# A 4096-node graph layer whose product A·y is made from seven block products for eight, with the additions on the vector engine and the masks on GpSimd

## The chip, the cores and the metric

The kernel runs on one core of a Trainium2 chip. Such a core has a matrix engine (PE in the profile, with its weight loads as PEld), a vector engine (DVE), a scalar engine (ACT), GpSimd (POOL) and a sync engine (SP), each with its own instruction stream, and 16 DMA engines that serve the queues of SP, ACT and POOL. Engines wait for each other by semaphores; within one engine the instructions run in the order in which they stand. The metric is the device time of one execution in microseconds (us). Time before: 2134.33 us, the median of three runs (2130.61 to 2136.05).

## What is computed

There are N = 4096 nodes with F = 512 features in f32. `adj` is a symmetric pattern with about 0.8% of its entries set and a full diagonal, the values being random and not symmetric.

```
# layer 0
h  = relu(layernorm(x))
d  = rowsum(adj) ** -0.5                      # 0 where the sum is 0
x1 = x + relu((d[:, None] * adj * d[None, :]) @ h @ W0 + b0)
# layer 1
g  = relu(layernorm(x1))
s  = g @ W1 @ a[:F]        t = g @ W1 @ a[F:]
e  = leaky_relu(s[:, None] + t[None, :], 0.2)
P+ = softmax(where(adj > 0, e, -1e12))        P- = -softmax(where(adj > 0, -e, -1e12))
out = x1 + elu(concat([P+ @ g, P- @ g], 1) @ Wtrans)
```

Layer 0 works on `adj` as a dense matrix. Layer 1 uses its pattern: for each block of 64 rows only those columns are gathered that have an entry there.

## The kernel before

**Tiles and groups.** Rows come in 32 tiles of 128. `y0[j] = d_j (h_j W0)` is kept in SBUF for all 32 tiles j. Layer 0 is then `acc_i = sum over j of adj[i, j] y0[j]`, with 128x128 blocks of the transposed `adj` as weights and 512 columns moving. Each f32 matmul is two PE instructions in the profile (two passes), each with its own weight load. The output tiles i are done in eight groups (`GROUPS`, start and count): (26,6), (16,4), (20,4), (0,4), (4,4), (8,4), (12,4), (24,2). I number them 0 to 7. Group 0 runs beside the preparation of `y0` (loading x, layernorm, transposes, the product with W0, the row sums of `adj`) and ends at about 342 us.

**A group (`group`, from line 914).** It goes through jp = 0..15, two tiles j at a time. `load_at` (L780) brings the columns of `adj` on SP's queue, 512 KB at a time: two j for a group of four, four j for the group of two. `multiply` (L790, matmul at L795) issues the products; in the last steps the products are ordered by output tile, so that the accumulators end one after the other. Four PSUM banks hold a group's accumulators, and there are enough banks for two groups.

**Masks (`pack`, L682).** From every `at` tile DVE makes a u8 mask `at > 0` (L692) and the maximum over each 64 columns (`flags`, L696), and POOL's queue writes the mask into tables in DRAM (L708), from which layer 1 gathers. `EARLY` names three groups whose masks are made earlier: in group 2 the tiles of (24,2), in group 3 those of (12,4) and in group 4 those of (8,4) are loaded a first time and masked. So groups 3 and 4 load and mask two tiles each jp, groups 1 and 2 their own (2 also the narrow ones), and 5, 6 and 7 mask nothing.

**Ends of groups (`finish0`, L715).** At jp = 0 of the next group, DVE evicts each accumulator (times d, plus bias), adds x, ACT and DVE make the layernorm `h` (L738 clears its padding on POOL first), two products with the vectors of `a` give s and t (L742), and the row `h` is written into eight tables: one by POOL's queue, seven by ACT's (`put_row`, L420). `h` has two buffers, four for the last but one group, (12,4), whose seven writes per tile are instead kept in `puts` and issued on SP's queue at the end of group 7.

**Lists.** In groups 3 and 5, `make_lists` turns the flags into keys at jp = 2 (`make_keys`), and list rounds on DVE (MAX8 at L375, MATCH_REPLACE at L377) follow, two or three a jp; they give the columns to be gathered. POOL puts the lists together by indirect DMAs (`join`, L390) and deals them out (`deal`).

**Group 7 and the verdict.** Beside the products of (24,2), the first pair of row blocks of layer 1 (pair 16) is begun: `gather0` issues 22 indirect DMAs on POOL (L428) at jp 4, 6 and 10; `weights0` makes the attention weights (scores at L440) and `product0` (L1014) the products. Then `finish0` ends the last two tiles, `judge` (L885) computes a verdict whether the lists hold everything, and a branch on it leads to `sparse_layer1` (L1075). Its PE products are at L1131 and L1154, its gathers again at L428.

**s.** The values of s go to DRAM (`spread_s`, L758) and come back broadcast to all partitions (`load_s`, L768) into eight tiles `s_bc` of 128x512, which stand in SBUF for the whole kernel.

**Order.** The program is written in the order of the work; a scheduler may move instructions of an engine against each other, except those that are held by `keep_in_program_order`. Tiles with several buffers (`bufs`) make a later writer wait for the last reader of the buffer.

Of the kernel before, what the change touches and what calls it, by code (L numbers as in the profile page):

```python
# [27 lines left out]
Y_PARTS = (8, 11, 13)  # L28
EPS = 1e-5
# [228 lines left out]
def gcn_gat_kernel(  # L258
# [21 lines left out]

    nc = tc.nc
# [47 lines left out]
    s_bc = [const.tile([P, 4 * P], F32, name=f"s_bc{k}") for k in range(NJ // 4)]  # L329
# [107 lines left out]
    def scores(r, z, t):  # L437

        n = z.shape[1]
        return nc.vector.tensor_tensor(  # L440
            z,
            t.to_broadcast([P, n, RB]),
            s_bc[r // 8][:, r % 8 * RB : (r % 8 + 1) * RB].unsqueeze(1).to_broadcast([P, n, RB]),
            ALU.add,
        )
# [16 lines left out]
    def tree(pool, r, q, half):  # L462

        t = pool.tile([P, half, 2 * RB], F32, tag="tree", name=f"tree{r}", bufs=1)
# [5 lines left out]
        total = pool.tile([P, 2 * RB], F32, tag="total", name=f"total{r}", bufs=3)  # L470
# [22 lines left out]
    with sbuf(name="y0", bufs=1) as y_pool, sbuf(name="wa", bufs=1) as wa_pool, sbuf(name="bits", bufs=2) as bits_pool, sbuf(name="small0", bufs=4) as small, ExitStack() as lists:  # L493
        list_pool = lists.enter_context(sbuf(name="list", bufs=1))
# [14 lines left out]
        flags = [list_pool.tile([P, EJ * NE, 2 * NH], F32, name=f"flags{g}") for g in range(2)]  # L509
# [7 lines left out]
        xs, hx_t, ars, parts, y0 = {}, {}, {}, {}, {}  # L517
        masks = {}

        def make_keys(g):  # L520
# [3 lines left out]
            kp = []  # L524
            for a in range(2):
                nc.vector.tensor_scalar(bits[:, a], flags[g][:, :, a::2], 0.0, None, ALU.is_gt)
                k2 = ps.tile([P, EN], BF16, tag="ps", name=f"kp{g}_{a}")
                for k in range(EJ):
                    nc.tensor.transpose(
                        k2[:, k * P : (k + 1) * P],  # L530
# [3 lines left out]
                kp.append(k2)  # L534
# [3 lines left out]
            for a in range(2):  # L538
                nc.vector.tensor_tensor(key[:, 2 * a], kp[a], rank, ALU.mult)
            nc.vector.tensor_tensor(key[:, 1], key[:, 0], kp[1], ALU.mult)  # L540
            for a in range(2):
                nc.vector.tensor_tensor(key[:, 2 * a], key[:, 2 * a], key[:, 1], ALU.subtract)
            one = make_pool.tile([P, EN], F32, tag="one", name=f"one{g}")
# [31 lines left out]
        def load_bias():  # L575
            b_row = small.tile([1, F], F32, tag="b_row", name="b_row", bufs=1)
            nc.scalar.dma_start(out=b_row, in_=b0)
            nc.gpsimd.partition_broadcast(b_bc, b_row)
# [13 lines left out]
        def weight_rows(a_sb, w1t):  # L592
# [5 lines left out]
            row = small.tile([2, F], F32, tag="wa_row", name="wa_row", bufs=1)  # L598
# [17 lines left out]
        def load_x(ln_pool, queue, j):  # L616
# [627 lines left out]
```

## Time and profile before

| | us |
|---|---|
| median of three runs | 2134.33 (2130.61 to 2136.05) |
| the profiled execution | 2154.16 |
| its span, first to last instruction | 2152.4 |
| PE busy in the span | 2071.5 |
| DVE, ACT, POOL busy | 1040.5, 409.4, 945.2 |
| products of layer 0 (L795), busy | 891.8 |
| products of layer 1 (L1131 and L1154), busy | 767.2 and 225.1 |
| last product of group 7 ends | 1057.7 |
| verdict | 1071.96 |
| first product of layer 1 | 1126.33 |

A row of the profile names the line, the engine, the operation, output and inputs, shape and type, the number of instructions, the busy time and the mean of one in ns, and then the idle time of that engine just before them with what ended it. Times of matmuls overlap, since they are pipelined, so PE's rate is read from the distance between starts rather than from the duration of one. In windows, each engine's busy time in a stretch stands with its number of instructions, then the granted PE clock as a share, the share of the DMA engines' time and GB/s. A wait is given as engine, output and line, what released it, total us, how often, and the longest. In a timeline, the start, the duration, and in brackets the idle time before with its releaser.

### The profile page before, as it was taken

What the parts mean: (1) busy time and instruction counts of PE and PEld (TensorE: products, weight loads), DVE (VectorE), ACT (ScalarE), POOL (GpSimd) and SP (SyncE); (2) the same over time, 40 slices, a digit from 0 to 9 for tenths busy, and PEclk for the clock granted to TensorE, in tenths of its full rate; (3) what the DMA queues carried; (4) which work ended last, traced back from release to release, by engine and by line L of the source; (5) the groups of instructions that cost most, each with busy time, mean ns of one, the idle gap of its engine ahead of it and who ended that gap; (6) DMA issues with size and microseconds to landing.
All of it is one profiled execution on the core that took longest, in us unless ns stands there. A gap on an engine that the chain in (4) does not pass through costs nothing.

```text
span 2152.4 us, 17006 instructions
## 1 busy us (share of the span) xinstructions
PE 2071.5 (96%) x5208; PEld 938.0 (44%) x5208; DVE 1040.5 (48%) x2429; ACT 409.4 (19%) x764; POOL 945.2 (44%) x1017
## 2 busy tenths in 40 slices
PE   7999999999999999999849999999999999999998
PEld 3443444444444444444324444444444444444443
DVE  5444524243498638912414635455444454454441
ACT  5545610000000000000112222112212212112111
POOL 2010002121213230232376677777777777777740
PEclk9999999999999999999979999999999999999999
DMA  9988928887865966283888878887878887888850
GB/s 367 372 303 327 359 91 302 260 289 227 303 223 198 309 207 222 83 268 126 296 260 261 255 231 250 245 241 240 246 239 241 249 240 236 244 246 241 244 172 21
DMA packets 186427, 523.86 MB, mean 243 GB/s; under 512 B 25683, under 2 KB 34995, under 8 KB 186326
## 3 DMA queue, kind: packets, MB, share of 16 engines
q0 software_dynamic: 73856, 283.61, 43.5%
q1 hardware_dynamic: 81728, 183.20, 24.7%
q10 hardware_dynamic: 30742, 55.88, 7.4%
q8 instruction: 42, 0.69, 0.1%
q14 instruction: 59, 0.48, 0.1%
HBM read 419.67 MB, written 102.92 MB: 243 GB/s over the span
## 4 chain that ended last, share of the span: by engine, by line
PE 85%; DMA 5%; issue 4%; DVE 2%; ACT 1%; POOL 1%; another core or an unknown queue 1%; DVEq 0%; POOLq 0%; ACTq 0%
PE u L1131 35%; PE acc L795 35%; PE o L1154 10%; DMA xt<-in_x 4%; PE yp L657 2%; PE tp L486 1%; PE u L1014 1%; DVE sta L410 0%; ACT ar L647 0%; DMA ar<-in_adj 0%; PE cs L476 0%; POOL g L428 0%; DMA ld<-dummy 0%; DMA g<-table,idx 0%
## 5 line engine op out<-in xcount | busy, mean ns | idle before, releaser
L795 PE MATMUL acc<-y,at 128*128 128x512 f32 x2048 | 891.8, 593 | 2.4 <-ACT y L680 2.4
L428 POOL DMA_INDIRECT g<-table,idx x704 | 751.6, 1068 | 281.6 <-issue 198.0
L1131 PE MATMUL u<-g,p 128*128 128x512 f32 x1736 | 767.2, 599 | 16.8 <-DVE p L460 12.1
L795 PEld LDWEIGHTS acc<-y,at 128*128 128x128 f32 x2048 | 385.8, 190 | 474.8 <-issue 469.3
L1131 PEld LDWEIGHTS u<-g,p 128*128 128x128 f32 x1736 | 327.2, 191 | 407.6 <-issue 393.2
L440 DVE TENSOR_TENSOR z<-g,s_bc 128x512 f32<-128x512 f32 (+1 forms) x128 | 79.6, 623 | 392.4 <-DMA g<-table,idx 357.3
L1154 PE MATMUL o<-wt_sb,ut 128*128 128x512 f32 x512 | 225.1, 592 | 0.5 <-ACT ut L490 0.5
L460 DVE SCALAR_TENSOR_TENSOR p<-g,p 128x384 f32<-128x384 uint8 (+1 forms) x256 | 143.4, 620 | 76.4 <-issue 40.6
L692 DVE TENSOR_SCALAR m<-at 128x1024 uint8<-128x1024 f32 (+2 forms) x142 | 88.5, 632 | 159.7 <-DMA at<-in_adj_t 154.2
L453 ACT ACTIVATE p<-z 128x896 f32<-128x896 f32 (+2 forms) x136 | 116.0, 903 | 203.2 <-issue 114.6
L708 POOL DMA_DIRECT2D table<-m x71 | 54.9, 774 | 226.2 <-DVE m L692 188.0
L657 PE MATMUL yp<-w_sb,hx_t 128*128 128x512 f32 x256 | 123.4, 628 | 19.9 <-ACT y L680 17.9
L1154 PEld LDWEIGHTS o<-wt_sb,ut 128*128 128x128 f32 x512 | 94.8, 190 | 107.8 <-issue 106.9
L1140 ACT ACTIVATE us<-u,rl 128x512 f32<-128x512 f32 x62 | 42.6, 687 | 447.6 <-issue 277.9
L390 POOL DMA_INDIRECT ld<-li,off x48 | 45.2, 942 | 160.0 <-DMA ld<-li,off 104.0
L647 ACT ACTIVATE ar<-ar 128x1024 f32<-128x1024 f32 x96 | 100.1, 1043 | 17.9 <-DMA ar<-in_adj 17.9
L657 PEld LDWEIGHTS yp<-w_sb,hx_t 128*128 128x128 f32 x256 | 50.7, 201 | 88.6 <-issue 60.5
L610 ACT ACTIVATE rrb<-rrb 128x1 f32<-128x1 f32 x32 | 5.9, 199 | 417.3 <-DVE rrb L609 352.8
L618 POOL DMA_DIRECT2D xt<-in_x x28 | 15.8, 565 | 153.9 <-ACT hx L614 129.2
L375 DVE MAX8 lst<-keys 128x8 f32<-128x512 f32 x120 | 79.4, 682 | 0.9
L377 DVE MATCH_REPLACE8 keys<-lst,keys 128x512 f32<-128x512 f32 x114 | 76.4, 673 | 0.0
L449 DVE SCALAR_TENSOR_TENSOR z<-z 128x896 f32<-128x896 f32 (+2 forms) x68 | 70.8, 1041 | 2.2
(149 smaller groups left out, 1058.0 us busy)
## 6 DMA issues: line engine op xcount, KB each, us to landing
at<-in_adj_t SPq DMA_DIRECT2D x136, 512.0 KB
ar<-in_adj SPq DMA_DIRECT2D x128, 512.0 KB
table<-h ACTq DMA_DIRECT2D x182, 258.0 KB
table<-m POOLq DMA_DIRECT2D x55, 256.0 KB
at<-in_adj_t SPq DMA_DIRECT2D x32, 384.0 KB
g<-table,idx POOLq DMA_INDIRECT x704
xr<-in_x POOLq DMA_DIRECT2D x32, 256.0 KB
x1d<-y POOLq DMA_DIRECT2D x32, 256.0 KB
```

Source lines behind the costliest of these rows:

```text
L375: nc.vector.max(top, keys[:, c, :])
L377: nc.vector.match_replace(keys[:, c, :], top, keys[:, c, :], 0.0)
L428: nc.gpsimd.indirect_dma_start(out=gt[:, k, :], out_offset=None, in_=table[2 * n // RPT], in_offset=bass.IndirectOffsetOnAxis(ap=idx[n // ...
L440: return nc.vector.tensor_tensor(z, t.to_broadcast([P, n, RB]), s_bc[r // 8][:, r % 8 * RB : (r % 8 + 1) * RB].unsqueeze(1).to_broadcast([ ...
L453: nc.scalar.activation(p[:, :, g, :], z, AF.Exp, scale=(1.0, -1.0)[g])
L460: nc.vector.scalar_tensor_tensor(e, m, 0.0, e, ALU.is_gt, ALU.mult)
L647: i = nc.scalar.activation(ar, ar, AF.Identity, accum_out=part[:, c : c + 1])
L657: nc.tensor.matmul(yp, hx_t[j][:, c * P : (c + 1) * P], w0_sb[:, c, :], start=c == 0, stop=c == FC - 1,)
L692: i = nc.vector.tensor_scalar(m, at, 0.0, None, ALU.is_gt)
L795: nc.tensor.matmul(a, at[:, c, it * P : (it + 1) * P], y0[j0 + c], start=j0 + c == 0, stop=j0 + c == NJ - 1,)
L1131: nc.tensor.matmul(u, p[:, k0 + k].rearrange("p g c -> p (g c)"), gt[:, k, :F].bitcast(F32), start=k0 + k == 0, stop=k0 + k == nk - 1,)
L1154: nc.tensor.matmul(po, ut[:, g, c, :], wt_sb[:, g * FC + c, :], start=g == 0 and c == 0, stop=g == 1 and c == FC - 1,)
```

## The change

**Products.** For groups 1 to 7, two tiles j and two tiles i make a 2x2 block problem: the blocks of `adj` are 128x128, and each `y0` tile is cut into two halves of 256 columns. `multiply_blocks` makes seven products of 256 columns in place of eight. Their operands are the blocks themselves and sums of them: `sum_at` makes four sums on DVE for each `at` tile, and `sum_y` makes four per jp once, in group 1 (it also alters the y0 tiles in place and fills `t` tiles). The results stand in 3.5 banks per column pair, seven banks for a group of four; `join_blocks` makes the output tiles from them at the group's end: one ACT copy and five DVE additions per pair, then the affine step in the old eviction's place. Group 0 keeps the plain products.

**Masks.** In groups 1 to 6 `pack` makes the mask by POOL's `tensor_scalar`; the maximum stays on DVE and is issued one step later. The flags are bf16.

**Buffers and order.** The `at` buffers are six in all in place of nine and two; in group 7 four in place of five. The `h` of (12,4) has three buffers in place of four. One tile is finished per jp (order 0, 2, 1, 3), and x for it is loaded beforehand. List rounds are two a jp (three in group 6), joins one a jp. In group 7 the gathers' parts 1, 2 and 0 come at jp 4, 7 and 10, in place of 2, 1 and 0 at jp 4, 6 and 10.

**s.** The `s_bc` tiles are gone. `s_pair` (for pair 16) is loaded on ACT's queue at jp 0 of group 7; in layer 1 `load_s` brings 256 KB for four pairs at a time on SP, two of them ahead of `wt_sb`.

```diff
-    s_bc = [const.tile([P, 4 * P], F32, name=f"s_bc{k}") for k in range(NJ // 4)]
...
-        def pack(i0, j0, at, pin=False):
+        def pack(pool, engine, i0, j0, at, pin=False):
...
-            i = nc.vector.tensor_scalar(m, at, 0.0, None, ALU.is_gt)
+            i = engine.tensor_scalar(m, at, 0.0, None, ALU.is_gt)
...
-            nc.vector.tensor_reduce(
+            return partial(
+                nc.vector.tensor_reduce,
...
+        def join_blocks(i0, n, acc, work):
+            ys = {}
+            for x in range(n // 2):
+                p16, p23, p45, p7 = acc[x]
+                j0, j1 = i0 + x, i0 + n // 2 + x
+                ys[j0], ys[j1] = y, v = [new_y(work, j, -1) for j in (j0, j1)]
+                w = work.tile([P, H], F32, tag="w", name=f"w{j0}", bufs=1)
+                nc.scalar.copy(y[:, :H], p16[:, :H])
+                nc.vector.tensor_tensor(w, p16[:, H:], y[:, :H], ALU.add)
+                nc.vector.tensor_tensor(y[:, H:], p45[:, H:], w, ALU.add)
+                def first(p23=p23, y=y):
+                    nc.vector.tensor_tensor(y, p23, y, ALU.add)
+                def second(p7=p7, w=w, p45=p45, v=v):
+                    two = "p (a f) -> p a f"
+                    nc.vector.tensor_tensor(w, p7, w, ALU.add)
+                    nc.vector.tensor_tensor(
+                        v.rearrange(two, a=2), p45.rearrange(two, a=2),
+                        w.unsqueeze(1).to_broadcast([P, 2, H]), ALU.add)
...
+        def sum_y(jp):
+            k = 0 if jp < T_PARTS[0] else 1
+            t = ty[jp] = t_tiles[k][:, jp - k * T_PARTS[0]]
+            ya, yb = y0[2 * jp], y0[2 * jp + 1]
+            sub = partial(nc.vector.tensor_tensor, op=ALU.subtract)
+            sub(t[:, 1], yb[:, H:], ya[:, H:])
+            sub(ya[:, H:], ya[:, H:], ya[:, :H])
+            sub(t[:, 0], yb[:, H:], ya[:, H:])
+            sub(t[:, 2], yb[:, :H], t[:, 0])
+        def sum_at(pool, at, n, name):
+            a = blocks_of(at, n)
+            q, w = a.shape[1], a.shape[4]
+            t = pool.tile([P, 4, q, w], F32, tag="sums", name=name)
+            op = nc.vector.tensor_tensor
+            op(t[:, 0], a[:, :, 0, 1], a[:, :, 1, 1], ALU.add)
+            op(t[:, 1], t[:, 0], a[:, :, 0, 0], ALU.subtract)
+            op(t[:, 2], a[:, :, 0, 0], a[:, :, 0, 1], ALU.subtract)
+            op(t[:, 3], a[:, :, 1, 0], t[:, 1], ALU.subtract)
+            return t
+        def multiply_blocks(acc, n, jp, at, t):
...
+            for x in range(n // 2):
+                p16, p23, p45, _ = acc[x]
+                product(x, p16[:, :H], a[:, q, 0, 0], ya[:, :H], True)
+                product(x, p16[:, H:], t[:, 1, q], s[:, 0], False)
+                product(x, p45[:, :H], a[:, q, 1, 1], s[:, 2], True)
+                product(x, p45[:, H:], t[:, 0, q], ya[:, H:], False)
+                product(x, p23[:, :H], a[:, q, 1, 0], yb[:, :H], True)
+                product(x, p23[:, H:], t[:, 3, q], yb[:, H:], False)
+                if not last:
+                    seventh(x)
...
-        def group(b, work, at_pool, early, step):
+        def group(b, work, at_pool, sum_pool, step, prod, n_h=2):
...
-            for jp in range(NJ // 2):
+            prepare(0)
+            for jp in range(NP):
+                if jp + 1 < NP:
+                    prepare(jp + 1)
                 if jp == 0:
-                    finish0(work, *pending)
-                    acc = [bank(f"acc{i0 + k}") for k in range(n)]
...
+                    ys = take(work)
+                    p7 = bank(f"p7_{i0}")
+                    acc = [
+                        [*(bank(f"p{k}_{i0 + x}") for k in (16, 23, 45)), p7[:, x * H : (x + 1) * H]]
+                        for x in range(n // 2)
+                    ]
+                multiply_blocks(acc, n, jp, ats[jp], sums[jp])
+                while marking:
+                    marking.pop(0)()
...
+                        marking.append(pack(bits_pool, nc.gpsimd, e0, 2 * jp, at))
+                if jp < pn:
+                    j = order[jp]
+                    h = work.tile([P, ROW_W], F32, tag="h", name=f"h{j}", bufs=n_h)
+                    finish0(work, j, ys.pop(j), h, prod)
...
-        with sbuf(name="work0", bufs=2) as work, sbuf(name="at", bufs=9) as at_pool, sbuf(name="early", bufs=2) as early:
+        with sbuf(name="work0", bufs=2) as work, sbuf(name="sums", bufs=3) as sum_pool, sbuf(name="at", bufs=6) as at_pool:
...
-                    for _ in range((2, 3)[b % 2 == 0] if jp > 2 else 0):
+                    for _ in range((2, 3)[b == 6] if jp != 2 else 0):
                         if listing:
                             listing.pop(0)()
+                    if joining:
+                        joining.pop(0)()
...
-        with sbuf(name="work2", bufs=2) as work, sbuf(name="at2", bufs=5) as at_pool, ...
+        with sbuf(name="work2", bufs=2) as work, sbuf(name="sums2", bufs=2) as sum_pool, sbuf(name="at2", bufs=4) as at_pool, ...
...
                 if jp == 4:
+                    gather0(1)
+                if jp == 7:
                     gather0(2)
-                if jp == 6:
-                    gather0(1)
...
-            group(len(GROUPS) - 1, work, at_pool, None, step)
+            group(len(GROUPS) - 1, work, at_pool, sum_pool, step, row_tile, 3)
...
+            wanted = list(dict.fromkeys(r // 8 for r in order))
+            for _ in range(2):
+                tc.keep_in_program_order(load_s(wanted.pop(0)))
             for a in range(3):
                 gather1(pairs[0], a)
...
                     weights(order[k + 2])
+                    if wanted and order[k + 2] % 8 == 7:
+                        load_s(wanted.pop(0))
```

## The prediction

> **What bounds the kernel now.** I read the busy shares first, then the chain that ended last, the windows by group, and the rows and waits at the places that the change touches. The shares and the chain's sum by engine:
>
> ```profile
> PE 2071.5 (96%) x5208; PEld 938.0 (44%) x5208; DVE 1040.5 (48%) x2429; ACT 409.4 (19%) x764; POOL 945.2 (44%) x1017
> PE 85%; DMA 5%; issue 4%; DVE 2%; ACT 1%; POOL 1%; another core or an unknown queue 1%; DVEq 0%; POOLq 0%; ACTq 0%
> ```
>
> PE is the bound. The changed stretch, groups 1 to 7 of layer 0, runs from about 341.7 us (end of group 0) to 1057.7 us. The chain there, and windows of groups 3 and 6 (PE, PEld, DVE, ACT, POOL busy, clock, DMA share, GB/s):
>
> ```profile
> 399.78 110.06 PE acc L795 x256
> 954.13 80.90 PE acc L795 x188
> ...
> 547.00:659.00 112.00, 112.00 (x286) 49.67 (x285) 88.20 (x221) 4.22 (x9) 20.78 (x33) 1.00 0.76 256
> 881.00:992.00 111.00, 111.00 (x261) 48.91 (x260) 37.66 (x95) 4.18 (x9) 29.13 (x42) 1.00 0.53 169
> ```
>
> 256 passes (each f32 matmul is two) take 110.06 us: 0.43 us each, no gap, at full clock. Seen from here, time falls one for one with PE's work until another engine is late. DVE has 24 us to spare in the fullest group, 73 in the emptiest. The rows I price with:
>
> ```profile
> L795 PE MATMUL acc<-y,at 128*128 128x512 f32 x2048 | 891.8, 593 | 2.4 <-ACT y L680 2.4
> L486 PE MATMUL tp<-ident,us 128*128 128x128 f32 x256 | 39.5, 278 | 18.1 <-issue 18.1
> L468 DVE TENSOR_TENSOR tree<-tree 128x256 f32<-128x256 f32 x64 | 26.7, 417 | 1.2
> L692 DVE TENSOR_SCALAR m<-at 128x1024 uint8<-128x1024 f32 x94 | 64.9, 697 | 140.9 <-DMA at<-in_adj_t 135.5 <-DMA table<-m 5.3
> L325 POOL CAST ident<-ident 128x128 bf16<-128x128 f32 x1 | 0.3, 280 | 0.0
> L496 POOL IOTA rank<- 128x512 f32 x1 | 0.6, 556 | 10.2 <-issue 10.2
> L708 POOL DMA_DIRECT2D table<-m x71 | 54.9, 774 | 226.2 <-DVE m L692 188.0 <-DVE mva L414 14.8 <-DVE rs L670 6.9
> ```
>
> **Step 1: PE's products.** Each pair of row tiles has 13 column pairs over the groups, 16 steps jp. Before: 13x16x8 = 1664 passes of 512 columns; the starts lie 0.4289 us apart, 713.7 us in all. After: 13x16x7x2 = 2912 passes of 256. No row has that width. The durations of 512 and 128 columns give a slope of (593-278)/384 = 0.82 ns a column; half of 0.4289 is 0.2145. I take 0.2155. The weight loads could forbid it: they take 190 ns each, but
>
> ```profile
> 1305.70 0.30 PEld L476 LDWEIGHTS cs<-ones,total 128*128 128x128 f32 x2
> ```
>
> shows two inside 0.30 us, so a new one may start after 0.11 us. Bounds: 0.2145 below, 0.297 (half of the whole duration) above; the period of 512 is the nearest row, so I stay low. 2912x0.2155 = 627.5 us: 86.2 saved, 79.5 in the six groups of four (109.8 to 96.5 us each, 6.03 a jp) and 6.6 in the last group. At the upper bound the products would take 865 us.
>
> **Step 2: DVE's adds.** A group of four gets 16 times four 256-column adds (start to start about 0.335 us): 1.4 us of each 6.03, 23 a group. sum_y adds the same once, all in group 1. The join adds per column pair one ACT copy and five DVE adds (three at 417, two 512 wide at 685 ns) in place of nothing; the affine takes the old eviction's place: +5 us a group. The masks leave DVE: 96 of 1024 (0.6 start to start) and 16 of 512, 32 of the large in each of groups 3 and 4, 16 in 1 and 2. Demand per group against 96.5 us of PE, in group 3: sums 23, join and affine 8, finish 4x3.3 = 13, 32 flags at 0.32 = 10, keys 8, 26 list rounds at 1.27 (a MAX8 of 682 ns, a load, a replace of 673) = 33: 95. The like gives about 80 in group 1 (six tiles, sum_y), 58 in 2, 92, 90 and 87 in groups 4 to 6 (up to 30 rounds, no masks in the last two). On average it fits. But DVE works in order: make_keys with the first rounds is a block of about 10 us at jp 2, and the last finish's dot waits for table writes (14 to 15 us from one put to the next that may follow, h having two buffers):
>
> ```profile
> DVE prod L742 <- DMA table<-h: 22.0, 3, 11.2
> POOL h L738 <- DMA table<-h: 77.5, 15, 8.3
> ```
>
> Before, nothing that PE needed stood behind these on DVE except evictions; now sum_at of the next pair does, and three buffers of sums (12 us) are its slack. Following program order, group 3's sums for jp 5 come about 5 us late, and in groups 4 to 6 the fourth tile's dot ahead of the sums for jp 5 or 7 costs 2 to 5 us each. I take 18 us for groups 1 to 6. Bounds: 0 to 3 if the writes land sooner, 60 if groups 3 to 6 run at DVE's rate with these waits uncovered (10 to 15 each).
>
> **Step 3: masks on POOL.** The trace has none. The nearest rows: CAST 128 columns in 280 ns, IOTA 512 in 556: 0.72 ns a column above the start, so 1024 take 0.9 us; 8x280 = 2.24 is the other end. I take 1.2. POOL in group 4 then has 32x1.2 + 16 mask writes x0.77 + about 20 us of rows and joins = 71 of 96.5: covered. The cover ends at 2.0 us a mask there and 2.3 in group 3. At 2.24 group 4 runs 8 us long; the flags reduce on DVE, which waits for the mask, then stalls the sums behind it. Below nothing: no gain beyond DVE's 64 us, counted already.
>
> One rule speaks against this step. DVE's 417 ns add was measured with no GpSimd arithmetic beside it. The Trainium skill, page "SBUF — State Buffer", section "SBUF: two separate sides", says that a DVE instruction with two SBUF inputs and a GpSimd instruction that reads SBUF exclude each other for the whole instruction. No row of this trace shows such a pair. By it 32 masks would hold the adds up by an estimated 0.4 us each, 13 us in each of groups 3 and 4, and the sum below would end some 20 us later.
>
> **Step 4: groups' ends, buffers, transfers.** The acc banks had been double; now seven of eight are one group's. The first column pair's join (2.6 us) lies beside the second pair's products of the last step only if DVE is on time; 0 to 1 us per boundary, in step 2's 18. The at buffers fall from 9+2 to 6, one load per jp (two in groups 3 and 4, three in flight ahead). The same bytes in 12% less time lift the DMA share from 0.76-0.86 to 0.87-0.98 (group 0 held 0.99), so loads need not be late; if in group 1 they are, 0 to 5 us. xr is loaded earlier on POOL: no wait. Joins, one a jp, only spread POOL's issues.
>
> **Step 5: the last group and the verdict.** Here I expect a loss. Three lines of before:
>
> ```profile
> 1009.51 0.54 POOL L420 DMA_DIRECT2D table<-h  x1 [2.67 <-issue]
> 1015.15 1.02 POOL L428 DMA_INDIRECT g<-table,idx  x1 [5.10 <-DMA table<-h]
> 1045.06 21.89 SPq L420 DMA_DIRECT2D table<-h  x28
> 1071.96 0.15 DVE L911 CAST verdict<-ok_ps 1x1 int32<-1x1 f32 x1 [0.28 <-PE ok_ps L908]
> ```
>
> The group starts at 1002.3; gathers of pair 16 start 12.9 us in, and the verdict falls 69.7 in. With h's buffers cut from four to three, h of tile 15 on POOL must wait for the seven table writes of the first tile (12). Those are on SP behind the load of the last at tiles, whose buffer is free when PE ends jp 7, about 24 us in. Seven writes of 0.78 us: issued and written at about 33. Then POOL makes h15, its put and (5.1 us later, as before) the first gather: 41 us in instead of 12.9. Queued behind h15 on POOL are all 22 gathers: 22x1.25 = 27.5, landing 6 to 7 later, at about 75; the weights from them stand on DVE ahead of the last verdict steps: verdict about 80 us in. So the 6.6 us of this group go, and 10.5 are added after them. Bounds: -6.6 if the writes land with the 24 and the gathers' chain is slack, +15.
>
> **Step 6: s in layer 1.** The 32 broadcasts that stood on ACT and SP in layer 0 go; a 256 KB load per four pairs comes on SP. The first two stand ahead of wt_sb (landed 1123 before, needed later) and weights(34) waits for one. Gathers take the time from verdict to 1126.33 anyway, so I take +2, bounds 0 to 8.
>
> **Sum.** -79.5 + 18 + 10.5 + 2 = -49 us. The profiled execution took 2154.16 us (span 2152.4), 20 above the median of 2134.33: the sum makes 2105 of it, and 2085 of the median.
>
> **Rivals.** (A) PE's stream is everything: DVE slack and the gathers' cover hold. -86 +0 to 6 gives 2048 to 2054. For it: averages of every engine fit. Against: in-order waits above. (B) DVE becomes the bound in groups 3 to 6 (95, 92, 90, 87 of 96.5 are a hair from it): step 2 at 40 to 60, and step 5's loss: 2105 to 2130. (C) Slower, by GpSimd: masks of 3 us and over make POOL the bound, since groups 3 and 4 hold 32 each: 64m+22+33 against 193 us, an excess of 54 us at m = 3.0, where the gain is gone, 86 at 3.5: about 2170. Against: no elementwise row of POOL is near 3 ns a column. (D) The change does not do what it says: a 256-column pass costs no half of a 512. At 0.245 us 2912 of them take 713.7 again; then step 5's and 6's loss makes it 2140 to 2147, and 0.26 some 2185. For it: PE spends 44% of its time in weight loads, and their number grows by 1.75. Against: the 0.30 row.
>
> **How the numbers follow.** Less than 0.3% (6.4 us) can't be told from no change here. Forecast, 2060 to 2105: 0.45. A: 0.14. B: 0.15. Between B and no change, 2128 to 2141: 0.05. C: 0.12, D: 0.09. Faster 0.74, same 0.05, slower 0.21. The range 2050 to 2150 reaches from A through B and the bottom of D; outside it lie the most of C, half of D and a little of A: under 0.2. The likeliest alone: 2060 to 2105.
>
> **What the profile after would show.** Step 1: one PE row of 256-column products, x2912 where none is missing, starts 0.215 apart, groups of 96 to 100 us. Step 2: PE's idle on DVE sums in groups 3 to 6, a few us each; DVE busy above 85 of 97 there. Step 3: POOL masks of 1.0 to 1.5 us, with flags waiting little; adds at 417 ns, longer if the rule holds. Step 5: the first gather of pair 16 about 40 us into the last group, after a POOL wait for table writes; the verdict 10 us later against its start. Step 6: layer 1's first weights waiting for s or not. The forecast is wrong if masks exceed 2 us, if a pass exceeds 0.23, or if PE's idle time in groups 3 to 6 is under 2 us in all.

## Result

The changed kernel takes 2301.77 us, the median of four runs (2292.57 to 2303.65), against 2132.47 us of the kernel before on the same chip: a ratio of 1.0785, 95% interval 1.0750 to 1.0821. It is 169 us slower where 49 us less were forecast. The profiled execution has a span of 2301.7 us; that of the kernel before, 2152.4 us, was taken from an execution some 20 us above its median, so the two spans lie 149 us apart and not 169.

The page's busy times and the chain by engine, of the changed kernel:

```profile
PE 2062.9 (90%) x6456; PEld 1212.3 (53%) x6456; DVE 1186.8 (52%) x2862; ACT 414.7 (18%) x779; POOL 1234.2 (54%) x1129
PE 41%; POOL 5%; DMA 4%; issue 2%; DVE 2%; ACTq 0%; ACT 0%; SPq 0%; DVEq 0%; POOLq 0%
```

PE was 96% busy and 85% of the chain; it is now 90% and 41% (the shares add up to little over half of the span, since the chain can be followed back only to 1049.6 us). Windows by group, for groups 1, 2, 4, 5 and 6 (columns as before: PE, PEld, DVE, ACT, POOL busy, clock, DMA share, GB/s); the boundaries are the ACT copies of the last join of each group, and group 3, from 593.4 to 753.1, is left out:

```profile
341.00:455.00 114.00, 101.63 (x444) 86.24 (x443) 67.87 (x189) 6.33 (x15) 69.26 (x56) 0.96 0.70 237
455.00:593.40 138.40, 112.89 (x451) 93.13 (x450) 54.63 (x151) 5.00 (x11) 83.54 (x61) 0.89 0.58 184
...
753.10:931.30 178.20, 122.18 (x452) 99.31 (x452) 98.28 (x253) 5.09 (x12) 115.88 (x77) 0.80 0.55 182
931.30:1032.50 101.20, 100.12 (x477) 85.33 (x476) 89.92 (x246) 4.83 (x11) 14.87 (x24) 1.00 0.59 191
1032.50:1141.30 108.80, 100.88 (x452) 86.46 (x451) 71.03 (x199) 4.96 (x11) 31.99 (x43) 0.95 0.49 159
```

The groups that make masks (1 to 4) take 114, 138, 160 and 178 us against 110 before; 5 and 6, which make none, take 101 and 109. No engine fills the slow groups: in group 4, the slowest, DVE is busy for 98 of 178 us, POOL for 116, and the DMA engines' share is 0.55. So the groups are held up by waits that follow each other in a ring. The groups of instructions that carry it, shapes kept apart:

```profile
L690 POOL TENSOR_SCALAR m<-at 128x1024 uint8<-128x1024 f32 x94 | 262.0, 2792 | 146.4 <-DMA at<-in_adj_t 135.5 <-DVE sums L854 5.8 <-DVE lst L376 3.9
L1037 DVE TENSOR_REDUCE flags<-m 128x16 bf16<-128x256 int32 x88 | 36.2, 412 | 183.2 <-POOL m L690 163.9 <-POOL h L779 19.4
L864 PE MATMUL p<-t,sums 128*128 128x256 f32 x832 | 267.1, 406 | 90.4 <-DVE sums L852 81.8 <-DVE sums L853 8.5
```

A mask on GpSimd takes 2.79 us. GpSimd waits 136 us for at tiles, DVE 164 us for masks, PE 90 us for sums: each for the one before. One turn of the ring in group 4, from the timelines of SP, POOL, DVE and PE:

```profile
842.68 0.88 SPq L811 DMA_DIRECT2D at<-in_adj_t  x2
848.30 0.87 POOL L391 DMA_INDIRECT ld<-li,off  x1 [4.49 <-DMA ld<-li,off]
849.24 2.80 POOL L690 TENSOR_SCALAR m<-at 128x1024 uint8<-128x1024 f32 x1
852.07 0.42 DVE L1037 TENSOR_REDUCE flags<-m 128x16 bf16<-128x256 int32 x1 [4.98 <-POOL m L690]
853.13 2.80 POOL L690 TENSOR_SCALAR m<-at 128x1024 uint8<-128x1024 f32 x1
855.97 0.42 DVE L1037 TENSOR_REDUCE flags<-m 128x16 bf16<-128x256 int32 x1 [1.35 <-POOL m L690]
857.69 0.41 DVE L851 TENSOR_TENSOR sums<-at 128x256 f32<-128x256 f32 x1
858.83 1.22 PE L864 MATMUL p<-t,sums 128*128 128x256 f32 x2 [4.04 <-DVE sums L852]
855.96 0.88 SPq L811 DMA_DIRECT2D at<-in_adj_t  x2
```

The last line is the next turn's pair of loads. SP issues two loads at 842.68. GpSimd is kept by a join that waits 4.49 us for the one before it, makes two masks, DVE takes flags from each as it comes, and only then stands the next step's sums; PE gets them at 858.83. The second mask, ended at 855.93, frees an at buffer, and SP issues the next two loads at 855.96. The turn is 13.3 us for a step that PE does in 6.03. In group 4 SP waited 80.1 us, 14 times, for masks before it issued loads.

What links the ring is the order of DVE's queue. The program names the flags of a step behind the sums of two steps later. As built they stand ahead of older sums. In group 2, the flags of step 2 (by the loads that the mask and the sums read) stand ahead of the last of the four sums of step 0:

```profile
448.70 0.42 DVE L1037 TENSOR_REDUCE flags<-m 128x16 bf16<-128x256 int32 x1 [3.00 <-POOL m L690]
449.04 0.48 DVE L854 TENSOR_TENSOR sums<-at,sums 128x256 f32<-128x256 f32 x1
```

In the turn of group 4 above, the two flags stand ahead of all four sums of the step that PE needs next, and the first of them belongs to the step after it (the second is of a tile that is marked only). The tile that the first marks sits in one of six buffers, whose last holder must be done first, so PE waits for a load, two masks and the flags for tiles that it needs only later or not at all. Whether more `at` buffers would have hidden the mask's price was not tried.

Each wait costs more than its length. PE's windows behind such a wait, in group 4 (the first pair of passes after a wait of 7.42 us starts at 822.27):

```profile
822.30:826.50 4.20, 4.20 (x10) 3.40 (x11) 2.43 (x6) 0.00 (x0) 1.25 (x1) 0.50 0.79 258
827.50:830.50 3.00, 3.00 (x15) 2.47 (x13) 2.45 (x7) 0.00 (x0) 3.00 (x2) 1.00 0.01 3
```

The granted clock is 0.50 for some 4 us after an idle time of 7.42 us, ten passes in 4.2 us, and 1.00 after that. Over all runs with block products, 94 of the 105 waits of 3.1 us or more in the products are followed by a first pair of 1.1 us or more (1.22 us is half clock), and 9 of the 55 waits of 1.5 to 3.1 us; 40 of these 55 by one of 0.70. The Trainium skill has this, page "TensorE: Matmul & The Clock Gate", section "Part 1: The HAM clock gate (the "warmup" mystery)": an idle window of about 3.4 us halves the clock until PE has been busy for about as long. The runs agree with it in the main.

The sum of the stretch of groups 1 to 7: 859.0 us = 627.5 (2912 passes at 0.2155) + 150.0 of idle time before products + 81.5 of rest. By the clock records of the trace PE was busy for 115 us of this stretch at a granted clock below full, which makes some 57 us of the rest; 66 small products make some 4, and the other 20 are not assigned. Of the idle time, 107.5 us are waits for sums and 35.8 for the first add of a join (`w`, four waits, the longest 16.4 us). Before it was 716. After its end the verdict comes 31.0 us later (14.3 before), and from the verdict to the end it is 1070.8 us (1080.4 before). So 143 of the 149 us between the two spans lie in the stretch.

### The profile page after: what moved, and what is told of

Same layout as the page of the kernel before. It is cut to its first block, busy times and chain, and to the rows that moved or that the text cites. A ratio compares the mean times of both kernels' runs of the same rounds, so it can differ in the third digit from the quotient of the medians.

```text
span 2301.7 us, 20151 instructions
## 1 busy us (share of the span) xinstructions
PE 2062.9 (90%) x6456; PEld 1212.3 (53%) x6456; DVE 1186.8 (52%) x2862; ACT 414.7 (18%) x779; POOL 1234.2 (54%) x1129
## 4 chain that ended last, share of the span: by engine, by line
PE 41%; POOL 5%; DMA 4%; issue 2%; DVE 2%; ACTq 0%; ACT 0%; SPq 0%; DVEq 0%; POOLq 0%
PE u L1279 27%; PE o L1302 8%; POOL g L429 5%; PE p L864 3%; DMA g<-table,idx 2%; PE tp L484 1%; DMA table<-h 1%; PE u L1149 1%; ACTq L421 0%; DMA xr<-in_x 0%; PE cs L474 0%; DMA ld<-li,off 0%; DVE z L441 0%; DVE prod L783 0%; PE u L1161 0%
## 5 line engine op out<-in xcount | busy, mean ns | idle before, releaser
L690 POOL TENSOR_SCALAR m<-at 128x1024 uint8<-128x1024 f32 (+1 forms) x110 | 286.1, 2607 | 153.3 <-DMA at<-in_adj_t 142.2
L864 PE MATMUL p<-t,sums 128*128 128x256 f32 x832 | 267.1, 406 | 90.4 <-DVE sums L852 81.8
L864 PE MATMUL p<-y,sums 128*128 128x256 f32 x832 | 267.4, 405 | 17.2 <-DVE sums L854 17.2
L864 PE MATMUL p<-y,at 128*128 128x256 f32 x832 | 263.3, 400 | 6.4 <-DVE y L749 5.0
L864 PEld LDWEIGHTS p<-t,sums 128*128 128x128 f32 x832 | 166.4, 204 | 127.2 <-DVE sums L852 93.2
L864 PEld LDWEIGHTS p<-y,sums 128*128 128x128 f32 x832 | 169.2, 204 | 46.5 <-DVE sums L854 20.1
L864 PEld LDWEIGHTS p<-y,at 128*128 128x128 f32 x832 | 167.4, 203 | 36.3 <-DVE y L749 7.1
L823 PE MATMUL acc<-y,at 128*128 128x512 f32 x384 | 176.5, 598 | 2.4 <-ACT y L678 2.4
L864 PE MATMUL p<-t,at 128*128 128x256 f32 x416 | 134.2, 406 | 36.0 <-DVE w L745 35.8
L823 PEld LDWEIGHTS acc<-y,at 128*128 128x128 f32 x384 | 71.0, 191 | 81.2 <-issue 78.0
```

The costliest lines, as they stand in the source:

```text
L690: i = engine.tensor_scalar(m, at, 0.0, None, ALU.is_gt)
L823: nc.tensor.matmul(a, at[:, 0, it * P : (it + 1) * P], y0[j], start=j == 0, stop=j == NJ - 1)
L864: i = nc.tensor.matmul(out, left[:, x * P : (x + 1) * P], right, start=jp == 0 and first, stop=jp == NP - 1 and (final or not first),)
```

## Experiments

The medians of the kernel before lay at 2132, 2151, 2151, 2151 and 2131 us in the sets of runs below, which were made on several chips; so each is compared by its ratio to the kernel before on the same chip.

### Masks back on DVE

```diff
-                    marking.append(pack(bits_pool, nc.gpsimd, i0, 2 * jp, ats[jp]))
+                    marking.append(pack(bits_pool, nc.vector, i0, 2 * jp, ats[jp]))
-                        marking.append(pack(bits_pool, nc.gpsimd, e0, 2 * jp, at))
+                        marking.append(pack(bits_pool, nc.vector, e0, 2 * jp, at))
```

> The changed kernel with the masks of groups 1 to 4 back on DVE, all else kept. Theory (the mask on GpSimd, 2.79 us each, with DVE's flags waiting for it in order, is what costs): DVE gets 19 us of masks back in groups 3 and 4 and 10 in groups 1 and 2, which makes it the bound at 112 to 115 us in 3 and 4; the groups take about 102, 100, 115 and 112 us in place of 114, 138, 160 and 178, so some 160 us go: about 2140 us. Rival (the sums' place in DVE's order and the six at buffers cost the time, whoever makes the masks): groups 3 and 4 stay at 140 us or more: 2200 or more.

Measured: 2168.94 us, ratio 1.0076 (1.0043 to 1.0108); groups 1 to 4 at 103, 113, 116 and 117 us. The theory's size was nearly met (it named 2140 on the first chip, a ratio of 1.003): nine tenths of the loss hangs on who makes the masks. But the kernel isn't faster than before. Group 2 has little work on DVE and still takes 113 us. Timeline of DVE in it:

```profile
513.75 0.69 DVE L690 TENSOR_SCALAR m<-at 128x1024 uint8<-128x1024 f32 x1 [4.01 <-DMA at<-in_adj_t]
514.82 0.41 DVE L851 TENSOR_TENSOR sums<-at 128x256 f32<-128x256 f32 x1
521.02 0.69 DVE L690 TENSOR_SCALAR m<-at 128x1024 uint8<-128x1024 f32 x1 [4.00 <-DMA at<-in_adj_t]
522.08 0.42 DVE L851 TENSOR_TENSOR sums<-at 128x256 f32<-128x256 f32 x1
```

Each step, DVE waits 4 us for the load of a tile that it needs now for its mask only, with this step's sums behind it (the tile's own sums come two steps later, by the order of the loads): the same ring with a shorter link, 7.3 us a step instead of 6.03.

### Masks on ACT

```diff
-            i = engine.tensor_scalar(m, at, 0.0, None, ALU.is_gt)
+            if engine is nc.scalar:
+                i = nc.scalar.activation(m, at, AF.Relu, scale=100.0)
+            else:
+                i = engine.tensor_scalar(m, at, 0.0, None, ALU.is_gt)
```

and `nc.scalar` in the two calls of `pack`.

> The changed kernel with the masks of groups 1 to 4 made by ACT (relu of 100 times the entry into u8, which is above 0 just where the entry is, entries lying in 0.05 to 1). Theory: ACT is busy 4 to 7 us a group; 32 masks at about 1.05 us (its 1024-column row) make 34: groups 1 to 4 at about 100 us each, so 190 us go: about 2110 us. Rival (ACT's queue is late, since its layernorm steps wait up to 20 us for table writes and the masks stand behind them, so flags and at buffers are late): groups 3 and 4 at 125 or more, 2150 to 2200 us.

Measured: 2167.89 us, ratio 1.0060 (1.0024 to 1.0095); groups 1 to 4 at 101, 110, 122 and 109. Neither expectation was quite met: it lies between them. A mask on ACT takes 1.05 us, ACT is busy for 24 to 38 us of these groups, and DVE has none of the masks' work left; yet the stretch takes 714.5 us against 716.7 with the masks on DVE. So the masks' work on DVE is not what bounds it.

### The kernel before, with its masks on GpSimd

```diff
-            i = nc.vector.tensor_scalar(m, at, 0.0, None, ALU.is_gt)
+            i = (engine or nc.vector).tensor_scalar(m, at, 0.0, None, ALU.is_gt)
```

with `engine=nc.gpsimd` in groups 1 to 4, and the flags one step later.

> The kernel before with only the masks of groups 1 to 4 moved to GpSimd, the flags on DVE issued one step later as in the change. Theory: 32 masks of 2.79 us and 22 to 33 us of other POOL work make 111 and 122 us in groups 3 and 4 against 110 of PE, but nothing that PE needs waits for POOL except through at buffers and evictions: 2135 to 2155 us. Rival (GpSimd masks cost as much by themselves as in the changed kernel, through at buffers that come free late): above 2200 us. Second rival (they hurt only beside the sums): 2133 us.

Measured: 2273.85 us, ratio 1.0549 (1.0506 to 1.0591). The theory fell, and so did the second rival; the first rival's size was met (by the ratio the time is 2250 us on the first chip, where it named more than 2200). The masks on GpSimd cost some 118 us, by the ratio, without any block product or sum. The flags were not held here, so how much of this is the price and how much the order is not separated. In the waits, and in PE's timeline:

```profile
DVE flags L935 <- POOL m L692: 286.2, 85, 27.7
```

```profile
674.17 0.62 PE L553 MATMUL o_ps<-count,before 128*16 128x3 f32 x18 [24.19 <-DVE count L546]
```

Here no sums stand behind DVE's waits, but the list work does, and PE has small products for the lists in its own queue among the large ones: 24 us in that one line. The `at` buffers come free late too, as the first rival has it: SP waited 344 us for masks between 335 and 1180 us, though PE only 18 us for `at` tiles. The links through which a late mask reaches PE are others, the late mask is the same.

### Flags one step later in the program

```diff
-                while marking:
-                    marking.pop(0)()
+                late_marks, marking = marking, []
+                while waiting:
+                    waiting.pop(0)()
+                waiting.extend(late_marks)
...
```

with one mask buffer more for it, two of the lists' tiles sharing theirs.

> The changed kernel, masks on GpSimd, but the flags of a step are issued one step later still (one mask buffer more for it, two of the lists' tiles sharing theirs). If the link from GpSimd to PE is DVE's in-order wait for the mask ahead of the sums, that wait has a step (6 us) more of slack and most of the stall in groups 1 and 2 and a third or more in 3 and 4 goes: 2210 to 2250 us. If POOL's own rate or the release of at buffers by the masks is the link, nothing changes: 2290 to 2305 us.

Measured: 2320.09 us, ratio 1.0775 (1.0744 to 1.0806). No change, and no test either: in group 2 the scheduler put the flags at the same places in DVE's queue, ahead of the last sum of two steps before, and in groups 3 and 4 ahead of the sums as well. It led to the next edit, which holds the order.

### The order held, with the masks on GpSimd, DVE and ACT

```diff
                 while marking:
-                    marking.pop(0)()
+                    tc.keep_in_program_order(marking.pop(0)())
```

(for DVE the masks too).

> The changed kernel, masks on GpSimd, but every flags instruction held on DVE in the order of the program, so behind the sums of the step after next instead of ahead of the sums two steps older (the scheduler had moved it there, and the run with later flags had left that order as it was). Theory (the loop buffer free, load, mask on GpSimd, flags, sums, products is what stretches a step): groups 1 to 4 fall from about 114, 138, 160, 178 us to 101, 103, 113, 124, the last two by GpSimd's own rate: some 150 us less than the changed kernel's ratio of 1.0785 to before, so a ratio near 1.01. Rival (GpSimd's rate and its late release of at buffers alone): ratio 1.055 or more.

> Masks on DVE as in the earlier run with them there, masks and flags held in the order of the program, behind the sums of the next step. If the order was what was left, group 2 falls from 113 to 98 and groups 3 and 4 to DVE's demand of 111 to 114 from 116 and 117: 20 to 25 us less, ratio 0.997. If DVE is simply full: no change, ratio 1.007.

> Masks on ACT as in the earlier run with them there, flags held in the order of the program. Theory (order): groups 1 to 4 from 101, 110, 122, 109 to 98, 98, 104, 102: about 40 us less, ratio 0.988. Rival (something else than the flags' place keeps the sums late, ACT's masks behind its waits for table writes or the lists): ratio 1.00 to 1.006.

Measured, with the two unheld runs for comparison (groups and stretch in us, of the profiled executions; PE's idle time before products, and the rest beyond it and 627.5 us of passes):

| masks on | order | ratio to before | groups 1 to 4 | stretch | PE idle | rest |
|---|---|---|---|---|---|---|
| GpSimd (the change) | scheduler's | 1.0785 (1.0750 to 1.0821) | 114, 138, 160, 178 | 859 | 150 | 82 |
| GpSimd | held | 1.0328 (1.0278 to 1.0379) | 112, 97, 132, 164 | 775 | 94 | 53 |
| DVE | scheduler's | 1.0076 (1.0043 to 1.0108) | 103, 113, 116, 117 | 717 | 52 | 38 |
| DVE | held | 1.0053 (1.0027 to 1.0079) | 105, 97, 113, 124 | 707 | 39 | 40 |
| ACT | scheduler's | 1.0060 (1.0024 to 1.0095) | 101, 110, 122, 109 | 715 | 51 | 36 |
| ACT | held | 0.9905 (0.9873 to 0.9938) | 101, 98, 116, 112 | 695 | 35 | 33 |

With the masks on GpSimd, the order alone is worth 4.6%, about 98 us, less than the 150 expected and more than the rival allows, since groups 3 and 4 stay at 132 and 164. There the rival's link shows: in group 4 SP waits 110 us, 16 times, for masks before it issues loads, and PE 11.9 us for `at` tiles themselves. Group 2 becomes nearly free of PE's waits for sums and takes 97 to 98 us in all three, 96.5 of them its passes. With the order held and the masks on ACT the kernel is faster than before: 2135.53 us against 2150.79, the best of all, though by under 1%. That is the forecast's sign, at less than half its size (20 us of 49, by the ratio). With the masks on DVE no gain is shown, as the two intervals overlap: group 2 falls to 97 us, but groups 3 and 4 take 113 and 124, of which DVE is busy for 97 and 105.

### Four buffers of h in the last group

On top of the masks on ACT with the order held:

```diff
-            group(len(GROUPS) - 1, work, at_pool, sum_pool, step, row_tile, 3)
+            group(len(GROUPS) - 1, work, at_pool, sum_pool, step, row_tile, 4)
```

> As the run before it, and four buffers of h in the last group instead of three. If the wait of the fourth tile's h for the first one's seven table writes is what moves the gathers of pair 16 and the verdict, the first gather starts some 15 us into the last group instead of 50, the verdict falls 70 to 75 us in instead of 90, and the time falls by 12 to 18 us more: ratio 0.981. If the gathers were covered anyway: no change against the run before it.

Measured: 2135.68 us, ratio 0.9923 (0.9898 to 0.9948): no change. The mechanism that the prediction named is there. In the changed kernel POOL's timeline has

```profile
1183.17 0.10 POOL L779 MEMSET h<- 128x3 f32 x1 [20.80 <-DMA table<-h]
1185.22 0.54 POOL L421 DMA_DIRECT2D table<-h  x1 [1.94 <-DVE prod L783]
1191.68 1.02 POOL L429 DMA_INDIRECT g<-table,idx  x1 [5.92 <-DMA table<-h]
```

50 us into the group that starts at 1141.3; with four buffers it is

```profile
997.34 1.22 POOL L429 DMA_INDIRECT g<-table,idx  x1 [2.55 <-PE p L867]
```

26 us in (start at 971.0). But the verdict falls only from 89.9 to 85.3 us after the group's start, PE's last group is 70 us instead of 61, and from the verdict to the end it takes 1076.7 us instead of 1074.0; of the earlier gathers nothing is left in the medians. The longer group holds four waits of PE, 9.3 us in all, before which the profile shows nothing that released it, and the other run's group has none of them; what made them is not shown.

### GpSimd's prices

Beside group 6 of the kernel with the masks on ACT and the order held, six instructions on 512 columns, four times each:

```diff
...
+                        if kind < 3:
+                            nc.gpsimd.tensor_scalar((u8, f32, bf16)[kind], src, 0.0, None, ALU.is_gt)
+                        elif kind < 5:
+                            nc.gpsimd.tensor_copy((f32, bf16)[kind - 3], src)
+                        else:
+                            nc.gpsimd.tensor_tensor(f32, src, other, ALU.add)
```

> Masks on ACT with the flags held, and beside group 6, where GpSimd has little to do, four times six GpSimd instructions on 512 columns of an at tile, into mask buffers that nothing reads: is_gt into u8, f32 and bf16, a copy into f32 and bf16, and an addition of two f32 tiles into f32. The 512-column mask took 1516 ns in the changed kernel. If the u8 output is what makes it dear, is_gt into f32 takes 0.6 to 0.9 us; if it is the comparison, the copies take 0.6 to 0.9 us and all three is_gt 1.5; if GpSimd's f32 arithmetic has this price, all of them take 1.4 us or more.

Measured, by shape:

```profile
L1061 POOL TENSOR_SCALAR probe<-at 128x512 f32<-128x512 f32 x4 | 6.2, 1556 | 0.0
L1061 POOL TENSOR_SCALAR probe<-at 128x512 bf16<-128x512 f32 x4 | 6.0, 1500 | 0.0
L1061 POOL TENSOR_SCALAR probe<-at 128x512 uint8<-128x512 f32 x4 | 6.0, 1500 | 7.4 <-DVE sums L857 7.3
L1065 POOL TENSOR_TENSOR probe<-at 128x512 f32<-128x512 f32 x4 | 5.0, 1253 | 0.0
L1063 POOL CAST probe<-at 128x512 bf16<-128x512 f32 x4 | 2.9, 717 | 0.0
L1063 POOL COPY probe<-at 128x512 f32<-128x512 f32 x4 | 2.5, 614 | 0.0
```

It is the operation, in this one run: a comparison takes 1.50 to 1.56 us whatever it writes, a copy 0.61. The prediction priced a comparison by rows of a cast and of an iota.

### List rounds away from the groups' ends

```diff
-                    for _ in range((2, 3)[b == 6] if jp != 2 else 0):
+                    for _ in range(3 if 4 <= jp < 14 else 0):
```

on the kernel with the masks on ACT and the order held.

> Masks on ACT with the flags held, and the list rounds three a step at steps 4 to 13 of groups 3 to 6 and none at the ends, in place of two or three a step at all steps but one. Theory (what PE still waits for is DVE's backlog of rounds in front of the joins at the ends of groups 3 and 4 and in front of sums): the waits of 5.3 and 7.2 us at those joins go, with 2 us of halved clock behind each; 10 to 20 us less than the same kernel without it, ratio 0.982 to 0.986. Rival (three rounds a step delay the sums in the middle of the groups as much): no change, ratio 0.99 to 0.993.

Measured: 2145.20 us, ratio 0.9979 (0.9956 to 1.0002), above what either expectation named and worse than 0.9905 without the edit. PE's timeline:

```profile
651.42 1.22 PE L867 MATMUL p<-t,at 128*128 128x256 f32 x2 [13.11 <-DVE w L748]
...
788.62 1.22 PE L867 MATMUL p<-t,sums 128*128 128x256 f32 x2 [10.05 <-DVE sums L855]
```

Group 4 falls from 112 to 99 us, and the join behind which PE waited 7.2 us (it is that of group 5, not of group 4 as the expectation has it) now costs 0.9. But the join of group 3 makes PE wait 13.1 us in place of 5.3, and group 5, where the second list begins, goes from 99 to 119. The rival's reason, sums delayed by rounds, is not what these two waits show. DVE was idle before both, and the chain leads back to POOL's queue:

```profile
645.69 0.83 POOL L391 DMA_INDIRECT ld<-li,off  x1 [3.67 <-DMA ld<-li,off]
646.53 1.61 POOL L701 DMA_DIRECT2D table<-m  x2
649.59 1.06 ACT L691 ACTIVATE m<-at 128x1024 uint8<-128x1024 f32 x1 [9.50 <-DMA table<-m]
650.94 0.42 DVE L748 TENSOR_TENSOR w<-p,y 128x256 f32<-128x256 f32 x1 [7.33 <-ACT y L747]
...
772.98 0.83 POOL L391 DMA_INDIRECT ld<-li,off  x1 [6.21 <-DMA ld<-li,off]
779.46 0.57 POOL L719 DMA_DIRECT2D xr<-in_x  x1
783.72 0.69 DVE L780 SCALAR_TENSOR_TENSOR y<-y,xr 128x512 f32<-128x512 f32 x1 [18.91 <-DMA xr<-in_x]
```

The joins of the list wait for each other on POOL. Behind them stand, the first time, the writes of masks, for which ACT's next mask waits 9.5 us with the join's copy behind it in ACT's queue, and the second time the load of x, for which DVE waits 18.9 us with sums behind it. So both waits come from POOL's chain of joins, which falls elsewhere when the rounds are moved: without the edit the last join of the first list is issued about when group 5 starts (764.98 against 764.7), here 21 us after it (772.98 against 752.2).

### The mask at the price that was assumed

The mask as a copy of each entry's top byte, which is above 0 just where the entry is:

```diff
+            if engine is nc.gpsimd:
+                i = nc.gpsimd.tensor_copy(m, at.bitcast(U8)[:, :, 3::4])
...
```

in the changed kernel as it is, and with the flags held as above.

> The changed kernel, its masks still on GpSimd and DVE's order as the scheduler made it, but the mask made by a copy of the top byte of each f32 entry (not 0 just where the entry is not) in place of the comparison. By the prices of the GpSimd instructions measured before, a copy of 1024 columns takes about 1.15 us against 2.79, which is the price that the prediction took. Theory (the comparison's price sets the length of the loop load, mask, flags, sums): about 100 to 150 us less than the changed kernel, ratio 1.005 to 1.03. Rival (the flags' place in DVE's order costs this whatever the mask's price): ratio 1.05 or more.

> The same copy on GpSimd, and the flags held on DVE in the order of the program. Theory (with the price and the order that the prediction assumed, the change gains, by less than predicted since the joins and the list rounds still make PE wait): ratio 0.985 to 0.995, as with the masks on ACT. Rival (GpSimd beside DVE's adds costs by itself): ratio 1.00 or more.

Measured: 2195.89 us, ratio 1.0301 (1.0275 to 1.0327), in the scheduler's order, and 2146.97 us, ratio 1.0080 (1.0052 to 1.0108), with the order held. The copy takes 1.09 us, a little less than the prediction's 1.2. So in the scheduler's order the price of the comparison is worth 4.8%, the order at the cheap price another 2.2%, and with both as they were assumed the change still loses 0.8%, 1.8% behind the masks on ACT. For the last of these the theory failed and the rival's number held; its reason, that GpSimd beside DVE's adds costs by itself, is shown in part. The 416 adds take 408 to 417 ns (means of their four rows) with the masks on ACT or DVE; with the copies on GpSimd and the order held the four rows have 471 to 531, 33 us more in all. DVE's and POOL's timelines of that kernel:

```profile
403.33 0.41 DVE L855 TENSOR_TENSOR sums<-sums,at 128x256 f32<-128x256 f32 x1
403.78 1.28 DVE L857 TENSOR_TENSOR sums<-at,sums 128x256 f32<-128x256 f32 x1
403.74 1.04 POOL L691 COPY late_m<-at 128x1024 uint8<-128x1024 uint8 x1 [1.41 <-DMA at<-in_adj_t]
```

The add that meets the copy ends 0.28 us after the copy does. These adds cover only part of the 136 us that group 4 alone still takes there (112 with the masks on ACT). On GpSimd the masks also stand behind the joins, for which POOL waits 33.4 us in that group, 11 times; how the rest divides was not separated.

## Why the prediction was wrong, by its steps

**Step 1, the passes: right.** Starts of 256-column pairs lie 0.431 us apart where PE does not wait, 0.2155 a pass, and group 2 with the order held takes 97 to 98 us, 96.5 having been computed. Rival D is out.

**Step 3, the masks: the step that failed.** It took 1.2 us a mask and named 2.24 as the other end; measured were 2.79. The error was to price a comparison by the nearest row in shape (a cast and an iota) rather than in operation; no row of before showed a comparison on GpSimd, so the upper end had no ground. Masks over 2 us were a sign of being wrong that the prediction had named. It also said that the cover ends where POOL is full, at 2.0 to 2.3 us, and rival C set the loss at 3.0 us and more. At 2.79 POOL is busy for only 116 of 178 us of group 4 and the loss is already 169 us: the price acts through a ring of waits, not through POOL's throughput, so the cover that was computed from busy times did not hold. Of the distance from the change (1.0785) to the best variant (0.9905), the operation with its engine is worth most: the masks on ACT alone give 1.0060.

**The order of DVE's queue: the assumption behind steps 2 and 3 that failed.** Both took the order of the program, flags one step behind. As built, flags stood ahead of older sums: in group 2 those of step jp+2 ahead of the last sum of step jp. Held in the program's order, they give back 4.6% with the comparison on GpSimd and 1.6% with the masks on ACT.

**Step 2, DVE's sums and waits: mis-sized.** It put 18 us, with an upper bound of 60. With the masks on ACT and the order held, where neither of the two errors above is left, PE's idle time is 34.5 us and the rest 33.1: 68 us. The idle time alone is nearly twice the term. What was left out is the half clock behind each wait of 3 us and more: by the clock records it makes some 18 of the 33.1 us, small products 4, and the rest is not assigned. The waits are in part where the step said: at the joins behind list rounds (5.3 and 7.2 us after groups 3 and 5) and at sums in groups 3 and 4 (4.0 us each at 574 and 758 us); one of 4.1 us is at the start of group 7 and one of 3.4 us is for a load.

**The rule on the shared port: right in direction.** What the prediction took from the Trainium skill, page "SBUF — State Buffer", section "SBUF: two separate sides", it weighed at some 20 us beside its sum; with the comparison the adds take 18 us more in all than at 414 ns, with the copy 33. For the copy the wait is the whole instruction, as the page says of such a pair: the add shown above ends 0.28 us after the copy. With the comparison it is not: an add that starts with a mask of 2.79 us ends 1.3 us after the mask's start, and the next two run at 0.41 us inside it:

```profile
803.89 2.79 POOL L690 TENSOR_SCALAR m<-at 128x1024 uint8<-128x1024 f32 x1 [0.99 <-DMA at<-in_adj_t]
803.98 1.25 DVE L851 TENSOR_TENSOR sums<-at 128x256 f32<-128x256 f32 x1
805.82 0.41 DVE L852 TENSOR_TENSOR sums<-sums,at 128x256 f32<-128x256 f32 x1
806.16 0.41 DVE L853 TENSOR_TENSOR sums<-at 128x256 f32<-128x256 f32 x1
```

**Step 4: wrong on two points.** The loads were late, not for bandwidth (the DMA share fell to 0.55) but because a buffer is given back only by its mask. And the joins, one a step on POOL, do more than spread its issues: each waits for the one before it, 4.49 us in the turn shown, with masks queued behind. At the groups' ends, where 0 to 1 us a boundary was put, PE waited 35.8 us for the joins' first adds in the changed kernel and 12.5 us in the best variant.

**Step 5, the last group: right in its mechanism, without worth.** The first gather came 50 us into the group (41 forecast), after a wait for table writes of 20.8 us, and the verdict 89.5 us in (80 forecast, 69.7 before). But the run with four buffers brought the gathers back and not the time: what is gained at the verdict does not arrive at the end. The 10.5 us of this term can't be told from nothing here.

**Step 6, s by parts: no cost seen.** From the verdict to the end it is 1070.8 us in the changed kernel, 1059.1 to 1091.8 in its variants and 1080.4 before. That scatter, between chips and executions, hides anything as small as the 2 us forecast.

## What to carry to other kernels

Before an operation is moved to another engine, find a row of that operation on that engine; a row of the same shape says little (on GpSimd a comparison took 2.5 times a copy). Read the order of each queue as it is built, not as the program is written: one instruction that waits for a slow engine, ahead of work that the matrix engine needs sooner, turned spare time into a ring of waits that no busy share showed. And count some 2 us on top of a stall of the matrix engine of 3 us and more, for the half clock after it (ten passes took 4.2 us where 2.2 is the full rate).

## What the runs showed of the hardware that was not expected

- GpSimd, 512 f32 columns: comparison 1.50 to 1.56 us into u8, bf16 or f32, addition of two tiles 1.25, cast 0.72, copy 0.61; comparison of 1024 columns 2.79, and the same in the kernel before without the sums beside it (2.785).
- A comparison of 1024 columns on GpSimd holds up a DVE add with two SBUF inputs only at its beginning: in the changed kernel 12 of the 17 adds that started in its first 1.05 us ended 1.31 to 1.34 us after the mask's start, and all 50 that started later in it took 0.38 to 0.43 us. A copy of 1.04 us holds such an add to its end: the add shown above ends 0.28 us after it, and 25 of the 26 adds that the copies delayed in the run with the scheduler's order ended about 0.3 us after theirs.
- ACT makes a 1024-column u8 mask by a scaled relu in 1.05 us; it was the idle engine here, with 5 to 6 us of work in a group of the changed kernel.
- PE's granted clock was 0.50 after most of its waits of 3.1 us and more, for some 4 us where it is shown above.
